# Measured durations in a list scheduler, one softplus table, and an addition by rows: the last two layers of a four-layer network

## The chip, the cores and the metric

The program runs on one core of a Trainium2 chip. A core has five engines that each take their instructions strictly in order: PE (TensorE, matrix products, which write to PSUM), DVE (VectorE), ACT (ScalarE, which evaluates functions from a loaded table), POOL (GpSimd) and SP (SyncE, which here issues the transfers). They wait for each other through semaphores. The metric is the device time of one execution in microseconds (us); lower is better.

## The reference, cut to what matters

Four layers work on four images of 192 channels and 56x56 pixels, all in float32. The first two are done in one stage of the kernel and are not touched. The third is a windowed attention with a gated feed-forward part, the fourth a selective scan over each image in four directions.

```python
# third layer: what follows the attention
def _hft(x, w, b):                       # depthwise 3x3 convolution as a gate
    ...
    return jax.nn.sigmoid(_dwconv3(a, w, b)) * x
z1, z2 = jnp.split(z, 2, axis=1)
z = z1 * _dwconv3(_ln_c(z2, sgn_g, sgn_b), sg_w, sg_b)
return x1 + _conv1x1(z, fc2_w, fc2_b)

# fourth layer
xs = jnp.stack([x_hw, x_wh, x_hw[..., ::-1], x_wh[..., ::-1]], axis=1)
x_dbl = jnp.einsum('kcd,bkdl->bkcl', x_proj_w, xs)
dts, Bv, Cv = jnp.split(x_dbl, [R, R + N], axis=2)
dt = jax.nn.softplus(jnp.einsum('kdr,bkrl->bkdl', dt_proj_w, dts) + dt_proj_b[None, :, :, None])
def step(h, inp):                        # N = 4 states a channel
    dt_t, u_t, B_t, C_t = inp
    h = jnp.exp(dt_t[..., None] * A) * h + dt_t[..., None] * B_t[:, :, None, :] * u_t[..., None]
    return h, jnp.einsum('bkdn,bkn->bkd', h, C_t)
y = ys[:, 0] + ys[:, 2, :, ::-1] + transposed(ys[:, 1]) + transposed(ys[:, 3, :, ::-1])
```

So every image is scanned along its rows forward and backward and along its columns forward and backward, and the four results are added up in `y`.

## The kernel before, in words

**The scheduler.** Both layers are written as many small generators (one for a chunk of rows, a window, a scan). Each yields, before a piece of work, the engine, an assumed duration, the tiles it takes and perhaps a table of ACT; then it issues the instructions. `Order.run` (from line 296) is a list scheduler that runs while the program is built: among all generators it takes the one whose next piece can start first by the assumed durations, plus 0.05 us times the generator's place in line, and advances that engine's assumed clock. The order of the instructions on each engine is thus fixed in the program, and the assumed durations do nothing but decide it. `on_dve(*n, ...)` assumes 0.08 + 0.00105 us times the elements, `on_pe(n)` 0.0019 us times the columns, `on_pool(n, each=...)` 0.2 + `each` times the elements.

**Layer 2** (the third layer; `layer2`). Bands of rows go through `front`, `quad` (attention of four windows) and `back`; chunks of eight rows go through `head` (the gate, with a depthwise convolution), `grow` (layer norms, L1195 and L1215, and the expansion, L1432) and `tail` (the second convolution, then the product L1497, PE's L1506 and the addition L1514). `dwconv` issues nine taps for each of two or three channel groups on DVE (L1341, L1343), one piece of work a tap.

**Layer 3** (the fourth layer; `layer3`). `begin(b, c)` takes a chunk of eight rows of image b: layer norm, projection (PE, L1821), the depthwise convolution as 18 matmuls with diagonal matrices (PE, L1851), SiLU, and `product` (PE, L1893), which makes dt, B and C for the two row directions and stores them. Once all chunks of an image are through, `begin_columns` calls `product` for the two column directions; its operand is a view of `u` that steps by 56 elements. `load` fetches these rows again (SP), `sizes` makes dt for two chunks at a time (PE L1985, ACT softplus L1997), `decay` spreads dt over four states by transfers (SP, L2023) and takes the exponential (ACT, L2031). `scan(t, h)` does one chunk for one half of the channels: du = dt u (DVE, L2046 by rows, L2049 by columns), three matmuls that spread it over the states (PE, L2056), three products with B (DVE, L2062), three scans (DVE, L2078), three products with C (POOL, L2085), the sum over the states (PE, L2101) and the addition to y (DVE, L2106, L2111 by rows and L2114 by columns). I call one such `scan` a half-step: an image has 56 (14 rows forward, 14 columns forward, 14 columns backward, 14 rows backward), the layer 224, counted from 0. `final(b, c)` is the last layer norm and output projection (L1770, L1789, L1929, L1940).

**The table of ACT.** A piece of work may name a table; the scheduler then issues a load of that table (L315) when it differs from the last. For softplus it names `softplus_and_others`. The built program of before holds, ahead of the softplus of L1997, 71 further loads at L1997's own line, which the compilation put there.

Of the kernel before, what the change touches and what calls it, by code (L numbers as in the profile page):

```python
# [19 lines left out]
B, C, H, W = 4, 192, 56, 56  # L20
HW = H * W
HALF = 96
CH = 448
# [302 lines left out]
    return "PE", 0.0019 * n, takes, None, ready  # L326


def on_dve(*n, takes=(), ready=None):
    return "DVE", sum(0.08 + 0.00105 * i for i in n), takes, None, ready  # L330


def on_scan(n, ready):
# [13 lines left out]


EXP_LN, GELU = "natural_log_exp_and_others", "gelu_and_others"
SILU, SOFTPLUS = "silu_and_others", "softplus_and_others"  # L350


def layers01(tc, x_in, packs, aps, dst):
# [723 lines left out]
def layer2(tc, src, packs, aps, dst):  # L1077
# [12 lines left out]
    with ExitStack() as ctx:  # L1090
# [242 lines left out]
        def dwconv(parts):  # L1333


            for t in range(9):
                yield on_dve(*(n * W for _, _, _, n, _, _ in parts))
                for dst, pad, i, n, wt, bias in parts:
                    x = pad[:, i + t // 3 : i + t // 3 + n, t % 3 : t % 3 + W]
                    if t == 0:  # L1340
                        nc.vector.tensor_scalar(dst, x, wt[:, 0:1], bias, ALU.mult, ALU.add)  # L1341
                    else:
                        nc.vector.scalar_tensor_tensor(dst, x, wt[:, t : t + 1], dst, ALU.mult, ALU.add)  # L1343
# [332 lines left out]
def layer3(tc, src, packs, aps, dst):  # L1676
# [8 lines left out]
    with ExitStack() as ctx:  # L1685
# [106 lines left out]
        def begin(b, c):  # L1792


            u = us[b % 2]

            yield lambda: (b, c) == (0, 0) or (gone("begun", b, c - 1) if c else gone("begun", b - 1, NCHUNK - 1))
            yield lambda: b < 2 or gone("scanned", b - 2)

            yield lambda: b == 0 or gone("multiplied", 8 * NSC * (b - 1) + 6 * c)  # L1800
            yield on_sp("row", "row")
            xl, xn = take("row"), take("row")
            nc.sync.dma_start(xl[:HALF], pixels(src[b])[:, :, c * CH : (c + 1) * CH])

            i = NCHUNK * b + c
            pad, above = pads[i % 2], pads[(i - 1) % 2]
            yield lambda: i < 2 or gone("convolved", i - 2)
            yield on_pool(200, 200)
            nc.gpsimd.memset(pad[:HALF, :, :, 0 : W + 2 : W + 1], 0.0)
            if c == 0:  # L1810
                nc.gpsimd.memset(pad[:HALF, :, 1], 0.0)
            else:
                nc.gpsimd.tensor_copy(pad[:HALF, :, 0:2, 1 : 1 + W], above[:HALF, :, 8:10, 1 : 1 + W])
            if c == NCHUNK - 1:
                nc.gpsimd.memset(pad[:HALF, :, 10], 0.0)
            yield from layer_norm(xl, xn, over=(xl,))

            def project(m):
                px = take()
                for k in range(2):  # L1820
                    nc.tensor.matmul(  # L1821
                        px[:HALF, :CH], inT[:, k, HALF * m : HALF * m + HALF], xn[:, k], start=(k == 0), stop=(k == 1)
                    )
                return px

            tiles = []
            for m in range(2):
                yield on_pe(2 * CH, "bank")
                tiles.append(project(m))
            for m in range(2):  # L1830
                yield on_act(CH)
                nc.scalar.activation(  # L1832
                    pad[:HALF, m, 2:10, 1 : 1 + W],
                    rows2(tiles[m][:HALF, :CH]),
                    AF.Identity,
                    bias=in_b[:, m : m + 1],
                )
                done(tiles[m])
            passed.add(("begun", b, c))
            y0, y1 = max(8 * c - 1, 0), 8 * c + (8 if c == NCHUNK - 1 else 7)  # L1840
            n = y1 - y0
            at = y0 - (8 * c - 1)
            px = slice(y0 * W, y1 * W)
            zt = None
            for h in range(2):
                pz = pc = None
                for t in range(9):
                    yield on_pe(n * W, *(("bank",) if t == 0 else ()), ready=order.end - 0.5 if t else None)
                    if t == 0:
                        pc = take()  # L1850
                    nc.tensor.matmul(  # L1851
                        rows2(pc[:HALF, : n * W]),
                        diag[:, h, t],
                        pad[:, h, at + t // 3 : at + t // 3 + n, t % 3 : t % 3 + W],
                        start=(t == 0),
                        stop=(t == 8),
                    )
                yield on_act(n * W)
                nc.scalar.activation(
                    u[:HALF, h, px], pc[:HALF, : n * W], AF.Identity, bias=w["c96.conv_b"][:, h : h + 1]  # L1860
                )
                done(pc)
                yield on_pe(2 * CH, "bank")
                pz = project(2 + h)
                yield on_act(CH, takes=() if h else ("gate",))
                if h == 0:
                    zt = take("gate")
                nc.scalar.activation(zt[:, h], pz[:HALF, :CH], AF.Identity, bias=in_b[:, 2 + h : 3 + h])
                done(pz)
            done(xn)  # L1870
            passed.add(("convolved", i))
            yield on_act(2 * n * W, 2 * CH, table=SILU)
            nc.scalar.activation(u[:HALF, :, px], u[:HALF, :, px], AF.Silu)
            nc.scalar.activation(zt, zt, AF.Silu)
            yield on_sp()
            nc.sync.dma_start(pixels(zmem[b])[:, :, c * CH : (c + 1) * CH], zt)
            done(zt)
            yield from product(b, 0, px, u[:, :, px])
            passed.add(("rows", b, c))

        def begin_columns(b, c):
            yield lambda: all(gone("rows", b, i) for i in range(NCHUNK))
            uv = us[b % 2].rearrange("p h (y x) -> p h x y", x=W)[:, :, 8 * c : 8 * c + 8]
            yield from product(b, 1, slice(c * CH, (c + 1) * CH), uv)
            passed.add(("columns", b, c))

        def product(b, o, px, u):

            n = px.stop - px.start
            yield on_pe(2 * n, "bank")  # L1890
            pp = take()
            for k in range(2):
                nc.tensor.matmul(pp[:40, :n], w["c128.xpT"][:, k, o], u[:, k], start=(k == 0), stop=(k == 1))  # L1893
            yield on_act(n, takes=("prod",))
            t = take("prod")
            nc.scalar.copy(t[:, :n], pp[:40, :n])
            done(pp)
            yield on_sp()
            nc.sync.dma_start(prods[b][o][:, px], t[:, :n])
            done(t)  # L1900
# [133 lines left out]
        def scan(t, h):  # L2034
# [5 lines left out]
            px = slice(c * SCH, (c + 1) * SCH)  # L2040
            yield lambda: t in sized and (2 * t + h == 0 or gone("multiplied", 2 * t + h - 1))
            dts, b_, c_ = sized[t]
            yield on_dve(SCH, takes=("du",))
            du = take("du")
            if o == 0:
                nc.vector.tensor_mul(du, dts[h], u[:HALF, h, px])  # L2046
# [20 lines left out]
            for j in range(3):  # L2067
                g = 3 * h + j
                yield lambda: (t, h, j) in decays and (head or (t - 1, g) in states)
                da, at = decays.pop((t, h, j))  # L2070
                yield on_scan(SCH, ready=max(at, ends[j]))
                sts.append(take("st"))
                r = slice(None, None, -1 if s else 1)
                first = 0.0
                if not head:
                    before = states.pop((t - 1, g))
                    first = before[:, 0:1] if s else before[:, SCH - 1 : SCH]
                nc.vector.tensor_tensor_scan(  # L2078
                    sts[j][:, r], da[:, r], tiles[j][:, :SCH][:, r], first, ALU.mult, ALU.add
                )  # L2080
                done(tiles[j])
                if not head:
                    done(before)
                yield on_pool(SCH, each=0.0021)
                nc.gpsimd.tensor_mul(da, sts[j], c_)  # L2085
                das.append(da)
                if last:
                    done(sts[j])
                else:
                    states[t, g] = sts[j]  # L2090
# [14 lines left out]
            if (o, s) == (0, 0):  # L2105
                nc.vector.scalar_tensor_tensor(  # L2106
                    y[:HALF, h, px], u[:HALF, h, px], d_sum[:, h : h + 1], sums, ALU.mult, ALU.add
                )
                started.add((t, h))
            elif o == 0:  # L2110
                nc.vector.tensor_add(y[:HALF, h, px], y[:HALF, h, px], sums)  # L2111
            else:
                yv = y[:HALF, h].rearrange("p (y x) -> p x y", x=W)[:, 8 * c : 8 * c + 8]
                nc.vector.tensor_add(yv, yv, rows2(sums, H))  # L2114
            done(py)
            added[b] += 1
            if o == 0 and s == 1 and h == 1:
# [54 lines left out]
```

## Time and profile before

| | us |
|---|---|
| median of three runs | 7017.2 |
| lowest and highest | 7013.4, 7018.1 |
| the profiled execution's own time | 7014.4 |
| its span | 7012.6 |
| layers 0 and 1: 0 to 2969 | 2969 |
| layer 2: 2969 to 4908 | 1939 |
| layer 3: 4908 to 7012.6 | 2105 |
| busy: PE, DVE, ACT, POOL | 5931.5, 5950.0, 2699.1, 1408.0 |
| table loads of ACT at L315 and at L1997 | 358 and 71 |

The boundaries of the layers are the times at which their weights are fetched. A group of instructions is shown with its line, engine, operation, tiles and shapes, its count, the busy time in us and the mean duration of one in ns; behind the last bar stands the idle time of its engine just before it and what ended it. Busy time counts overlap once, so it can be less than count times mean. A float32 matmul shows as two records of PE.

### The profile page before, as it was taken

To read this page: it belongs to the slowest core of one execution; us is meant where nothing else is said; L and a number is where in the kernel's file an instruction comes from. 1 tells how busy PE (TensorE), PEld (TensorE's weight loads), DVE (VectorE), ACT (ScalarE), POOL (GpSimd) and SP (SyncE) were. 2 spreads that over 40 slices of the span, in tenths; PEclk is the share of its full clock that TensorE was granted. 3 is DMA by queue.
4 is the path that set the end of the run, shared out by engine and by line. 5 is a ranking of instruction groups with operands and counts; after the bars stand their busy time and mean duration, and the time that the engine had idled before them with its cause. 6 is when DMAs were issued, how large, how long until landed. Compare 5 with 4: busy or idle time off the path is not lost.

```text
span 7012.6 us, 107574 instructions
## 1 busy us (share of the span) xinstructions
PE 5931.5 (85%) x43810; PEld 2703.5 (39%) x43810; DVE 5950.0 (85%) x7379; ACT 2699.1 (38%) x4134; POOL 1408.0 (20%) x1409
## 2 busy tenths in 40 slices
PE   4999989999999994877888888875888999888856
PEld 2444444444544441344444454442322322222212
DVE  2799999999999999548999989997269779698697
ACT  1111111222212221144455555553356666566544
POOL 0000000000000000032222122210235445355354
PEclk9999989999999997989999999997999999999977
DMA  3222112221222112210000000000246555465454
GB/s 93 56 52 68 31 32 60 52 68 29 63 51 66 35 43 70 64 32 16 17 20 15 19 16 19 18 13 7 60 116 152 135 130 147 115 151 147 118 131 112
DMA packets 252043, 462.68 MB, mean 66 GB/s; under 512 B 30388, under 2 KB 237964, under 8 KB 240412
## 3 DMA queue, kind: packets, MB, share of 16 engines
q1 hardware_dynamic: 251548, 455.80, 25.6%
q8 instruction: 345, 5.65, 0.3%
q14 instruction: 150, 1.23, 0.1%
HBM read 238.58 MB, written 62.96 MB: 43 GB/s over the span
## 4 chain that ended last, share of the span: by engine, by line
DVE 47%; PE 36%; issue 7%; ACT 5%; POOL 2%; DMA 2%; SPq 0%; DVEq 0%; POOLq 0%; ACTq 0%
DVE pr L789 9%; DVE oa L794 6%; PE a_bank L634 5%; DVE bg L1343 5%; PE c_bank L1851 4%; DVE ob L794 4%; DVE st L2078 3%; DVE bxn L1343 3%; PE c_bank L2056 2%; PE a_bank L884 2%; PE a_bank L869 2%; PE c_bank L1893 2%; PE c_bank L2101 2%; DVE c_bank L2062 2%; PE c_bank L1929 2%
## 5 line engine op out<-in xcount | busy, mean ns | idle before, releaser
L789 DVE TENSOR_TENSOR pr<-vdx,attn 112x1792 f32<-112x1792 f32 (+4 forms) x720 | 1185.9, 1649 | 19.0
L634 PE MATMUL a_bank<-qk_in,w_a 64*49 64x392 f32 x9408 | 1158.6, 496 | 0.0
L2085 POOL TENSOR_TENSOR da<-st,bc 128x448 f32<-128x448 f32 x672 | 845.4, 1267 | 884.9 <-DVE st L2078 793.7
L794 DVE TENSOR_TENSOR oa<-oa,pr 112x1792 f32<-112x1792 f32 (+1 forms) x423 | 765.1, 1809 | 0.0
L634 PE MATMUL a_bank<-qk_in,wd 64*49 64x392 f32 x4032 | 694.6, 496 | 0.0
L2078 DVE TENSOR_TENSOR_SCAN st<-da,st,c_bank 128x448 f32<-128x448 f32 x576 | 644.7, 1133 | 20.9 <-issue 12.7
L634 PEld LDWEIGHTS a_bank<-qk_in,w_a 64*49 64x49 f32 x9408 | 431.7, 120 | 395.9 <-issue 391.2
masks.py:197 POOL MEMSET b_ident<- 128x128 f32 x1 | 0.2, 206 | 2861.2 <-DVE sc L1042 2861.2
L2031 ACT ACTIVATE da<-da,a_neg 128x448 f32<-128x448 f32 x672 | 407.4, 658 | 155.8 <-DMA da<-dt 144.6
L315 ACT ACT_TABLE_LOAD x358 | 459.3, 1283 | 6.2
L2062 DVE TENSOR_TENSOR c_bank<-c_bank,bc 128x448 f32<-128x448 f32 x672 | 385.3, 619 | 75.3 <-PE c_bank L2056 74.5
L2056 PE MATMUL c_bank<-du,w_c 32*128 32x448 f32 x1344 | 291.3, 663 | 173.9 <-DVE du L2049 96.4
L1343 DVE SCALAR_TENSOR_TENSOR bg<-bzpad,w_b,bg 128x448 f32<-128x448 f32 (+2 forms) x672 | 421.8, 682 | 0.0
L1851 PE MATMUL c_bank<-pad,diag 128*96 128x448 f32 (+2 forms) x1008 | 413.0, 549 | 2.4 <-ACT pad L1832 2.4
L2101 PE MATMUL c_bank<-da,w_c 128*32 128x448 f32 x1344 | 343.8, 612 | 73.9 <-POOL da L2085 60.3
L794 DVE TENSOR_TENSOR ob<-ob,pr 112x1792 f32<-112x1792 f32 (+3 forms) x282 | 393.3, 1395 | 0.0
L869 PE MATMUL a_bank<-xc,w_a 128*128 128x448 f32 x672 | 300.8, 577 | 70.2 <-DVE xc L854 70.2
L878 ACT ACTIVATE hm<-a_bank,w_a 128x448 f32<-128x448 f32 x168 | 106.4, 634 | 644.9 <-PE a_bank L869 619.1
L634 PEld LDWEIGHTS a_bank<-qk_in,wd 64*49 64x49 f32 x4032 | 249.1, 120 | 256.4 <-issue 254.5
L1432 PE MATMUL bank<-bxn,w_b 128*128 128x448 f32 (+2 forms) x672 | 295.0, 567 | 16.7 <-DVE bxn L1215 16.3
L884 PE MATMUL a_bank<-hm,w_a 128*96 128x448 f32 x672 | 289.3, 562 | 21.1 <-ACT hm L878 21.1
L586 ACT ACTIVATE qk_in<-a_bank,qk_bias,qk_scale 64x224 f32<-64x224 f32 (+5 forms) x288 | 146.3, 526 | 412.2 <-PE a_bank L571 409.9
(306 smaller groups left out, 10091.6 us busy)
## 6 DMA issues: line engine op xcount, KB each, us to landing
da<-dt SPq DMA_DIRECT2D x672, 224.0 KB
vdx<-vmem SPq DMA_DIRECT2D x168, 476.0 KB
bc<-prod SPq DMA_DIRECT2D x224, 224.0 KB
row<-x SPq DMA_DIRECT2D x56, 336.0 KB
x<-x SPq DMA_DIRECT2D x4, 2352.0 KB
vmem<-vt SPq DMA_DIRECT2D x56, 168.0 KB
xc<-x SPq DMA_DIRECT2D x56, 168.0 KB
mid<-xc SPq DMA_DIRECT2D x56, 168.0 KB
```

What stands on the lines that cost most here:

```text
L315: self.nc.scalar.preload_act_table_set(table)
L634: nc.tensor.matmul(py[a][outs[g], : 7 * W].rearrange("p (y x) -> p y x", x=W), wt[halves[a], dx], q[halves[a], r, i0 + m : i0 + m + 7, dx ...
L789: nc.vector.tensor_mul(pr, vv, wt)
L794: nc.vector.tensor_add(og, og, before)
L869: nc.tensor.matmul(ph[:, :CH], w["a128.c1T"][:, k, 128 * m : 128 * m + 128], xt[:, k], start=(k == 0), stop=(k == 1),)
L1343: nc.vector.scalar_tensor_tensor(dst, x, wt[:, t : t + 1], dst, ALU.mult, ALU.add)
L1851: nc.tensor.matmul(rows2(pc[:HALF, : n * W]), diag[:, h, t], pad[:, h, at + t // 3 : at + t // 3 + n, t % 3 : t % 3 + W], start=(t == 0), ...
L2056: nc.tensor.matmul(tiles[j][:, :SCH], w["c96.rep"][r], du[r], start=True, stop=True)
L2062: nc.vector.tensor_mul(tiles[j][:, :SCH], tiles[j][:, :SCH], b_)
L2078: nc.vector.tensor_tensor_scan(sts[j][:, r], da[:, r], tiles[j][:, :SCH][:, r], first, ALU.mult, ALU.add)
L2085: nc.gpsimd.tensor_mul(da, sts[j], c_)
L2101: nc.tensor.matmul(py[32 * j : 32 * j + 32, :SCH], w["c128.sum"], das[j], start=True, stop=True)
```

## The change

Five durations that the scheduler assumes are altered; for 448 elements, a tap of a depthwise convolution goes from 0.550 to 0.618 us, du from 0.550 to 0.752 (rows) and 0.886 (columns), the product with C from 1.141 to 1.275, a column product on PE from 1.70 to 3.40. The table named for softplus is `softplus`, so that the load at L315 is the one that the activation needs. And the addition of the column results to y walks along the rows of y: y is read and written in runs of eight neighbouring elements, while the sums in PSUM are read with a step of 56 elements; before, y stepped by 56 and the sums were read straight.

```diff
-def on_dve(*n, takes=(), ready=None):
-    return "DVE", sum(0.08 + 0.00105 * i for i in n), takes, None, ready
+def on_dve(*n, takes=(), ready=None, each=0.00105):
+    return "DVE", sum(0.08 + each * i for i in n), takes, None, ready
...
-SILU, SOFTPLUS = "silu_and_others", "softplus_and_others"
+SILU, SOFTPLUS = "silu_and_others", "softplus"
...
             for t in range(9):
-                yield on_dve(*(n * W for _, _, _, n, _, _ in parts))
+                yield on_dve(*(n * W for _, _, _, n, _, _ in parts), each=0.0012)
...
-            yield from product(b, 0, px, u[:, :, px])
+            yield from product(b, 0, px, u[:, :, px], 2)
...
-            yield from product(b, 1, slice(c * CH, (c + 1) * CH), uv)
+            yield from product(b, 1, slice(c * CH, (c + 1) * CH), uv, 4)
...
-        def product(b, o, px, u):
+        def product(b, o, px, u, passes):
...
-            yield on_pe(2 * n, "bank")
+            yield on_pe(passes * n, "bank")
...
-            yield on_dve(SCH, takes=("du",))
+            yield on_dve(SCH, takes=("du",), each=0.0018 if o else 0.0015)
...
-                yield on_pool(SCH, each=0.0021)
+                yield on_pool(SCH, each=0.0024)
...
-                yv = y[:HALF, h].rearrange("p (y x) -> p x y", x=W)[:, 8 * c : 8 * c + 8]
-                nc.vector.tensor_add(yv, yv, rows2(sums, H))
+
+                yv = y[:HALF, h].rearrange("p (y x) -> p y x", x=W)[:, :, 8 * c : 8 * c + 8]
+                nc.vector.tensor_add(yv, yv, sums.rearrange("p (x y) -> p y x", y=H))
```

Since one line is added, the lines of the new kernel from 2113 on stand one lower.

## The prediction

> **What bounds the kernel now.** I first split the span by layer, in the view of busy time per stretch (columns: length; then busy us and instructions of PE, PE weight loads, DVE, ACT, POOL; granted PE clock; DMA share; GB/s). The first three lines are the layers; the other three are one image of the last layer: rows backward, rows forward of the next image, and its two column passes.
>
> ```profile
> 0.00:2969.00 2969.00, 2642.63 (x23294) 1285.26 (x23294) 2690.30 (x2135) 573.96 (x1061) 13.23 (x13) 0.95 0.22 54
> 2969.00:4908.00 1939.00, 1516.69 (x15012) 868.31 (x15012) 1663.13 (x3258) 942.13 (x1414) 453.28 (x619) 0.89 0.07 19
> 4908.00:7012.60 2104.60, 1772.17 (x5504) 549.94 (x5504) 1596.57 (x1987) 1183.00 (x1659) 941.47 (x777) 0.91 0.49 126
> ...
> 5409.00:5555.00 146.00, 133.13 (x421) 45.55 (x418) 107.84 (x139) 100.50 (x142) 62.30 (x50) 0.96 0.54 141
> 5555.00:5694.00 139.00, 126.43 (x366) 37.83 (x368) 94.77 (x123) 73.65 (x101) 54.30 (x52) 0.95 0.47 119
> 5694.00:5890.00 196.00, 169.83 (x590) 49.99 (x588) 189.66 (x231) 121.36 (x174) 110.31 (x90) 0.94 0.58 147
> ```
>
> The first layer is untouched. Layer 2 is DVE's (1663 of 1939 us). Layer 3 changes its bound twice an image: in the column passes DVE is busy 97% (189.7 of 196), in the row passes PE is (133 of 146, 126 of 139) while DVE idles about 80 of 285 us. Next, who DVE waits for, first in layer 2, then in layer 3 (total us, times, longest):
>
> ```profile
> DVE bxn L1215 <- ACT bank L1213: 40.3, 15, 5.5
> DVE bp L1514 <- PE bank L1506: 40.1, 26, 4.5
> DVE bacc L1655 <- PE bank L1639: 40.0, 18, 4.8
> DVE bzpad L1215 <- ACT bank L1213: 23.8, 11, 4.9
> ...
> DVE y L2106 <- PE c_bank L2101: 134.0, 25, 24.1
> DVE c_bank L2062 <- PE c_bank L2056: 74.5, 76, 8.0
> DVE row L1789 <- ACT c_bank L1787: 71.1, 22, 8.4
> ```
>
> All are waits for a chain through PE and ACT that the list scheduler thought covered. Then the groups of instructions that the diff names, and two pieces of the chain that ended last:
>
> ```profile
> L1343 DVE SCALAR_TENSOR_TENSOR bg<-bzpad,w_b,bg 128x448 f32<-128x448 f32 x480 | 299.7, 679 | 0.0
> ...
> L1997 ACT ACT_TABLE_LOAD x71 | 91.1, 1283 | 4.0 <-DVE st L2078 3.6
> ...
> L2049 DVE TENSOR_TENSOR du<-dt,u 96x448 f32<-96x448 f32 x112 | 113.6, 1014 | 0.0
> L2114 DVE TENSOR_TENSOR y<-y,c_bank 96x448 f32<-96x448 f32 x112 | 109.9, 982 | 12.9 <-PE c_bank L2101 12.6
> L2111 DVE TENSOR_TENSOR y<-y,c_bank 96x448 f32<-96x448 f32 x56 | 34.0, 607 | 30.6 <-PE c_bank L2101 30.6
> ...
> 5624.88 24.91 PE c_bank L1893 x32
> ...
> 5650.40 1.28 ACT L315
> ...
> 5651.69 1.28 ACT L1997
> ...
> 5652.98 0.64 ACT dt L1997
> ```
>
> A tap counts 299.7/480 = 0.624 us of DVE though one lasts 679 ns: neighbours overlap. The column products stand in one block of 24.91 us on PE (32 records: 14 column matmuls and 2 row matmuls, two records each), in which DVE waits 22.9 us. Behind it two table loads stand in a row before softplus.
>
> [...] The trace has the 1283, but the activation starts 0.01 us after the load, so I count 1.283. [...] du by columns, one hopping source, takes at best 947 ns, (947-140)/448 = 1.80; y by columns, source and destination hopping, 982 ns is 1.88 (140 ns is what L2111's 607 leaves over 448 x 1.042). Those streams are in SBUF. [...] No DVE instruction of the trace hops through PSUM.
>
> **The change, part by part.**
>
> *Taps in layer 2.* No instruction changes; the planner's 448-element tap goes from 0.08+0.00105x448 = 0.550 to 0.618 us, against 0.624 measured. The built order shows DVE's sequence with other interleaving. I summed the DVE work that stands in the order between a layer norm's subtraction and its multiplication, between the last product and L1514, and between the softmax's subtraction and L1655, by the durations above. In each class I took the length of chain at which the shortfalls of the old order add up to the waits measured between 3140 and 4650 us (23.9, 18.4, 19.1, 31.9 us; chains of 4.6 to 7.7 us), and applied it to the new order: layer norms lose about 10 us of shortfall, L1514 3.5, L1655 3; the reload after L1416 gains 3. With 6 us at the layer's two ends that is -20 us. Bounds: -40 (the shortfalls don't see that a wait removed also brings the next chain forward) and +10 (PE's own order is shuffled too).
>
> *Softplus table.* 71 loads of 1.283 = 91 us leave ACT, and the built order has 6 fewer switches besides. ACT is busy 1183 of 2105 us in layer 3, so only loads on the chain count: ten whole ones stand on it and three tails of 0.15, 13.3 us. What lies beside them takes over in part (DVE's scans, PE's convolution): -10, between 0 and -13.3.
>
> *y by rows.* 112 additions now hop in PSUM only; y is read and written in runs of 8. [...] They all stand in the column passes, which DVE bounds, but where the order has an addition as the last thing between du and L2062, PE's broadcast (du to L2062 took 1.4 to 2.3 us) swallows the saving; 70% gives -5. Ends: a free hop, 0.607 us, 112 x 0.375 = -42[...]. [...]
>
> *du, C products and column products in the planner.* du goes from 0.550 to 0.752 and 0.886 (0.856 and 1.014 measured), the C product on POOL from 1.141 to 1.275 (1.258), a column product from 1.70 to 3.40 us ((24.91-4x0.43)/7 = 3.31 measured). Durations change order, not work. In the built order the seven column products stand in one block at the same half-step (each image has 56: 14 rows forward, 28 columns, 14 rows backward), so the 22.9 us wait stays. What moves is the next image's convolution. Counting matmuls of one image (half-steps 70 to 126 of the layer's 224), the column passes hold 57 of L1851 before and 50 after; the rows backward 36 and 45. At 0.864 us each (18 records of the chain in 7.78 us; so for the other projections too, with 0.96 us for three broadcasts, 0.88 for three sums, 0.75 for a dt matmul and 3.31 for a column product) PE's work goes from 158 to 150 us in the column passes, where it was hidden by DVE, and from 128 to 138 us in the rows backward, where PE is the bound. It also stands in longer blocks: half-steps 97 and 98 hold 26.8 us of PE against 14.7 of DVE (before: 12.9 and 12.6), half-step 117 has 18 convolution matmuls in it. Taking the larger of PE's and DVE's work half-step by half-step, the sum grows by 9 us an image, 27 us over three. For the row passes of before this sum gives 286 us against 285 measured; for the columns it is too strict (209 against 196). So +16, between 0 and +27. No wait is added; the DMA issues of SP (L2023, L1970) keep their number; ACT waits 144.6 us for them in the layer, beside DVE's work.
>
> Sum: -20-10-5+16 = -19. The profiled execution took 7014.4 us around its span of 7012.6; the median of the runs is 7017.2, 2.8 higher. 7017.2-19 = 6998.
>
> **The rivals.** *The PSUM hop is free* (chance 0.26): y takes 0.61 us, -42 x 0.7 = -29 instead of -5, 6974. For it: the additions of L1655 read and write runs of 8 at 409 ns, no dearer than L1594's long ones at 410, so y itself is free of penalty. [...] *The blocks on PE decide* (0.25), the slower end: in half-steps 97-98 and 116-117 the excess of PE over DVE grows by 11.8 and 8.5 us, thrice each, 61 us if nothing is caught up later; against the 35 us of gains, +26, 7043. It decides from 5.8 us a block on. For it: DVE can't run ahead of PE by more than the next scans, and y L2106 waits behind just such a block today. Against it: the half-steps after are lighter. *Nothing that can be told* (0.07): the waits of layer 2 move rather than shrink and the rest cancels, 7015.
>
> **How the numbers follow.** My case has 0.42, with a range of its own from 6980 to 7013 us. A measurement of this kernel can tell about 0.2%, 14 us, from no change: faster ends at 7003, slower begins at 7031. My case is faster by 0.62 of its chance, the free hop by 0.95, together 0.51; slower is 0.85 of the blocks' case and a little of mine, 0.22; the rest, 0.27, is the same. Range: from 6955 (free hop, and layer 2 at its -40) to 7045 (blocks not caught up).
>
> **What would show it.** ACT with 71 loads fewer at L1997's line and none in a pair; y by columns at 0.9 us (0.6 if the hop is free, over 1 if the forecast fails there); DVE's waits in layer 2 for L1213, L1506 and L1639 20 us smaller; the column passes shorter by 2 to 3 us an image and the rows backward longer by 5 or so; L2106's wait behind the block still 23 us. It is wrong if layer 2 is not shorter than 1939 us, or if the row passes grow by more than 10 us an image.

## The result and the profile after

The changed kernel took 6990.8 us in the median (6988.4 to 6993.5, five runs) against 7017.2 us for the kernel before (7013.4 to 7022.3): 0.9963 of its time, 95% interval 0.9948 to 0.9978. That is 26 us less, 7 us below the 6998 forecast and inside its range. The forecast's sum was 19 us; the terms that make it up were not all right.

The profiled execution took 6988.4 us around a span of 6986.6. First the changed kernel's busy time per stretch, by layer, with the columns of the prediction (length; busy us and instructions of PE, weight loads, DVE, ACT, POOL; granted PE clock; DMA share; GB/s):

```profile
0.00:2969.50 2969.50, 2649.49 (x23294) 1283.69 (x23294) 2689.76 (x2135) 573.24 (x1061) 13.22 (x13) 0.95 0.22 54
2969.50:4909.10 1939.60, 1503.62 (x15012) 864.54 (x15012) 1671.73 (x3258) 940.57 (x1412) 443.96 (x619) 0.89 0.07 19
4909.10:6986.60 2077.50, 1763.92 (x5504) 540.16 (x5504) 1538.24 (x1987) 1091.34 (x1584) 947.80 (x777) 0.92 0.50 128
```

Layer 2 gained nothing (1939.0 to 1939.6). All of the gain is in layer 3, 2104.6 to 2077.5: DVE has 58 us less there, ACT 92 us less. To see which phase gained I cut layer 3 at du: a column pass runs from the first du by columns of an image to its first du of the backward rows (half-steps 14 to 41 of an image), a row pass from there to the next image's first du by columns. One image of the kernel before, columns and then rows:

```profile
5212.90:5409.30 196.40, 170.22 (x592) 50.32 (x592) 190.48 (x233) 121.84 (x175) 110.69 (x91) 0.95 0.59 148
5409.30:5693.60 284.30, 258.86 (x782) 82.92 (x780) 201.91 (x260) 173.86 (x241) 116.20 (x100) 0.96 0.50 130
```

and of the changed kernel:

```profile
5215.10:5404.30 189.20, 159.34 (x563) 46.21 (x563) 179.82 (x232) 114.54 (x169) 111.88 (x88) 0.92 0.61 152
5404.30:5696.40 292.10, 266.58 (x815) 85.41 (x812) 196.96 (x261) 156.29 (x227) 118.31 (x102) 0.95 0.49 127
```

The columns became 7.2 us shorter: DVE has 10.7 us less to do. The rows became 7.8 us longer: PE has 7.7 us more to do, the convolution that the columns no longer hold. Over the first three images the columns give 22 us and the rows take back 18 (the means stand in the table below). Most of the profit comes from the last image: its column pass and what follows went from 203.0 + 150.3 to 185.6 + 144.1 us.

The groups of the changed kernel that answer to those of before (count, then busy us, mean ns):

```profile
L315 ACT ACT_TABLE_LOAD x352 | 451.6, 1283 | 6.0
L1343 DVE SCALAR_TENSOR_TENSOR bg<-bzpad,w_b,bg 128x448 f32<-128x448 f32 x480 | 301.3, 682 | 0.0
...
L2049 DVE TENSOR_TENSOR du<-dt,u 96x448 f32<-96x448 f32 x112 | 113.1, 1010 | 0.0
...
L2115 DVE TENSOR_TENSOR y<-y,c_bank 96x448 f32<-96x448 f32 x112 | 67.7, 604 | 21.3 <-PE c_bank L2101 21.1
...
L2111 DVE TENSOR_TENSOR y<-y,c_bank 96x448 f32<-96x448 f32 x56 | 33.9, 606 | 45.7 <-PE c_bank L2101 45.7
```

The addition by columns, which reads PSUM with a step of 56 elements, takes 604 ns, as long as the one by rows that reads it straight (606); it was 982. The 71 table loads at the softplus's own line are gone, and L315 has the 6 fewer that the built order showed.

DVE's waits in layer 3 of the changed kernel (total us, times, longest):

```profile
DVE y L2106 <- PE c_bank L2101: 121.9, 22, 23.8
DVE c_bank L2062 <- PE c_bank L2056: 115.6, 89, 8.1
```

The wait behind the block of seven column products is still there, 23.8 us. The wait for the broadcast of du grew from 74.5 to 115.6 us. And DVE's waits in layer 2 of the changed kernel:

```profile
DVE bxn L1195 <- PE bank L1193: 62.1, 15, 28.0
DVE bp L1514 <- PE bank L1506: 37.8, 22, 4.8
DVE bxn L1215 <- ACT bank L1213: 34.1, 19, 4.8
DVE bzpad L1215 <- ACT bank L1213: 28.8, 13, 7.9
DVE bzpad L1195 <- PE bank L1193: 21.7, 7, 6.5
DVE bacc L1655 <- PE bank L1639: 20.5, 13, 3.6
...
DVE bacc L1308 <- ACT bacc L1306: 12.0, 10, 4.2
DVE bg L1341 <- ACT bzpad L1467: 11.2, 16, 1.7
```

beside the lines of before that the prediction did not show:

```profile
DVE bxn L1195 <- PE bank L1193: 56.1, 15, 27.8
...
DVE bzpad L1195 <- PE bank L1193: 12.6, 8, 2.5
...
DVE bacc L1308 <- ACT bacc L1306: 5.2, 8, 1.3
...
DVE bg L1341 <- ACT bzpad L1467: 2.6, 3, 0.9
```

The wait for L1639 is halved and those for L1213 and L1506 fall by 1.2 and 2.3 us, but those for L1193, L1306 and L1467 rise by 31 us together and take it over.

### The profile page after: what moved, and what is told of

Its sections match the earlier page's. It is cut to its first block, busy times and chain, and to the rows that moved or that the text cites. A ratio compares the mean times of both kernels' runs of the same rounds, so it can differ in the third digit from the quotient of the medians.

```text
span 6986.6 us, 107490 instructions
## 1 busy us (share of the span) xinstructions
PE 5917.0 (85%) x43810; PEld 2688.4 (38%) x43810; DVE 5899.7 (84%) x7379; ACT 2605.1 (37%) x4057; POOL 1405.0 (20%) x1409
## 5 line engine op out<-in xcount | busy, mean ns | idle before, releaser
L794 DVE TENSOR_TENSOR oa<-oa,pr 112x1792 f32<-112x1792 f32 (+1 forms) x423 | 764.8, 1808 | 0.0
L2062 DVE TENSOR_TENSOR c_bank<-c_bank,bc 128x448 f32<-128x448 f32 x672 | 382.7, 618 | 116.3 <-PE c_bank L2056 115.6
L2101 PE MATMUL c_bank<-da,w_c 128*32 128x448 f32 x1344 | 360.5, 601 | 93.1 <-POOL da L2085 82.5
L1343 DVE SCALAR_TENSOR_TENSOR bg<-bzpad,w_b,bg 128x448 f32<-128x448 f32 (+2 forms) x672 | 423.9, 686 | 0.0
L1851 PE MATMUL c_bank<-pad,diag 128*96 128x448 f32 (+2 forms) x1008 | 406.5, 545 | 0.2 <-ACT pad L1832 0.2
L794 DVE TENSOR_TENSOR ob<-ob,pr 112x1792 f32<-112x1792 f32 (+3 forms) x282 | 393.1, 1394 | 0.0
L2056 PE MATMUL c_bank<-du,w_c 32*128 32x448 f32 x1344 | 261.2, 642 | 124.2 <-DVE du L2049 68.8
```

What stands on the lines that cost most here:

```text
L794: nc.vector.tensor_add(og, og, before)
L1851: nc.tensor.matmul(rows2(pc[:HALF, : n * W]), diag[:, h, t], pad[:, h, at + t // 3 : at + t // 3 + n, t % 3 : t % 3 + W], start=(t == 0), ...
L2062: nc.vector.tensor_mul(tiles[j][:, :SCH], tiles[j][:, :SCH], b_)
L2101: nc.tensor.matmul(py[32 * j : 32 * j + 32, :SCH], w["c128.sum"], das[j], start=True, stop=True)
```

## The experiments

Each kernel is timed against the kernel before on the same chip. The table has the phases of layer 3 from one profile each: the mean of the first three column passes and of the three row passes, the last column pass together with what follows it, and PE's granted clock in the last column pass. Conv is the count of convolution matmuls (L1851) in half-steps 70 to 97 (columns), 98 to 111 (rows backward) and 112 to 125 (rows forward) of the built order.

| | us | ratio, 95% | columns | rows | last columns + rest | clock there | conv |
|---|---|---|---|---|---|---|---|
| before | 7017.2 | 1 | 196.6 | 285.5 | 353.3 | 0.74 | 57, 36, 33 |
| the change | 6990.8 | 0.9963 (0.9948-0.9978) | 189.2 | 291.5 | 329.7 | 0.86 | 50, 45, 31 |
| y alone | 6989.4 | 0.9952 (0.9939-0.9964) | 191.0 | 285.9 | 343.0 | 0.86 | 57, 36, 33 |
| table alone | 7016.4 | 0.9995 (0.9987-1.0003) | 197.0 | 285.8 | 355.7 | 0.72 | 57, 36, 33 |
| y, table | 6976.0 | 0.9937 (0.9924-0.9949) | 189.7 | 281.6 | 355.6 | 0.62 | 57, 36, 33 |
| du, C, column durations | 7039.5 | 1.0024 (1.0014-1.0033) | 197.4 | 296.3 | 342.4 | 0.87 | 50, 45, 31 |
| taps alone | 7021.2 | 1.0003 (0.9994-1.0011) | 196.7 | 288.0 | 353.8 | 0.73 | 57, 36, 33 |
| eight taps | 6973.4 | 0.9938 (0.9923-0.9953) | 196.7 | 288.0 | 354.3 | 0.73 | 57, 36, 33 |
| y, table, du, columns | 6929.0 | 0.9870 (0.9857-0.9884) | 182.6 | 279.6 | 331.8 | 0.84 | 60, 36, 30 |
| y, table, du | 6947.3 | 0.9895 (0.9881-0.9908) | 189.7 | 281.3 | 323.1 | 0.89 | 39, 54, 33 |
| y, table, spread | 6945.1 | 0.9892 (0.9878-0.9905) | 194.6 | 270.0 | 356.9 | 0.67 | 54, 45, 27 |
| the change, C 0.0023 | 6950.6 | 0.9906 (0.9891-0.9921) | 181.7 | 282.3 | 344.9 | 0.81 | 60, 36, 30 |
| the change, C 0.0025 | 6918.7 | 0.9862 (0.9845-0.9878) | 183.6 | 272.9 | 332.2 | 0.82 | 63, 36, 31 |
| spread, du, columns, C 0.0025 | 6832.1 | 0.9740 (0.9726-0.9755) | 183.5 | 255.6 | 327.0 | 0.92 | 56, 36, 24 |

Three kernels of the table leave layer 3 as it was (before, taps alone, eight taps), and their rows took 285.5, 288.0 and 288.0 us: a difference of 2 or 3 us between two profiles says nothing.

**The parts apart.** Four kernels with one part or two, the rest as before. Their edits are hunks of the change: the last one (y), the one of SOFTPLUS (table), both, and those of du, the C product and the column products (the three durations).

> The kernel before with the addition of the columns by rows alone; the order of the instructions is that of before. Theory A (the addition gives the gain and the new order takes part of it back): the addition takes 0.604 us as in the changed kernel, 112 x 0.378 = 42 us of DVE, of which 70 to 90% reach the end: 29 to 38 us faster, about 6983, the column passes 189 us or less instead of 196.5, the row passes unchanged at 284. Theory B (the new durations give the gain, the addition's saving is swallowed by the wait for PE's broadcast): at most 10 us faster.

> The kernel before with the softplus table alone; order as before, 71 table loads fewer. Both theories: 10 us faster (0 to 13), in the row passes and at the start of layer 3; ACT's busy time falls by 91 us. Rival: all of it is covered, no difference.

> The addition by rows and the softplus table, with all durations of the scheduler as before. Theory A: the sum of the two single runs, 39 to 48 us faster than before and thus 10 to 20 us faster than the changed kernel, 6970 to 6980, since the row passes keep their 284 us or less where the changed kernel has 292. Theory B: slower than the changed kernel, 6998 or more.

> Only the scheduler's durations of du, C product and column product, with the old addition, the old table and the old taps. Theory A: 9 convolution matmuls an image move from the column passes into the rows backward, three times, each half-step excess uncovered: 10 to 25 us slower, the row passes 292 us instead of 284, the column passes no longer than before. Theory B: 10 to 20 us faster.

Beside these four the kernel before took 7020.9 us. The addition by rows alone gives 31.5 us. Its group, in the profile of that kernel:

```profile
L2114 DVE TENSOR_TENSOR y<-y,c_bank 96x448 f32<-96x448 f32 x112 | 67.6, 604 | 18.9 <-PE c_bank L2101 18.9
```

112 x (0.982 - 0.604) = 42.3 us leave DVE, and three quarters of it (31.5/42.3 = 0.74) arrive in the time. They don't arrive evenly: DVE loses 10.6 us an image, and the first three column passes become 5.7 us shorter each, the last one 11.7, with PE's clock at 0.86 there instead of 0.74. The table alone can't be told from no change (4.4 us); on top of y it is worth 6989.4 - 6976.0 = 13.4 us. In the profiles this is a balance: 25 us are gained up to the last column pass, and 12.6 are lost in it and after it (343.0 to 355.6), where the clock falls from 0.86 to 0.62. The three durations cost 18.6 us. So y and table without any new duration are 15 us faster than the whole change, and the new order of layer 3 takes back part of what they give.

**Taps alone.** Is layer 2's part lost, or taken back elsewhere?

```diff
-                yield on_dve(*(n * W for _, _, _, n, _, _ in parts))
+                yield on_dve(*(n * W for _, _, _, n, _, _ in parts), each=0.0012)
```

> Only the planner's duration of a tap in layer 2 is changed; the order of layer 3 is as before, and so is every instruction. Theory 1 (formed after the result: the waits for L1639 and L1213 shrink, but the layer's end still comes after the same chain of head, projections and tail, so the time goes into other waits): layer 2 stays within 5 us of 1939 us, the kernel within 5 us of the one before, ratio 0.9993 to 1.0007. Theory 2 (the prediction's own step: 20 us less waiting of the vector engine is 20 us less time, and in the changed kernel something else took it back): layer 2 at 1919 us, ratio 0.9972.

No difference: 7021.2 us against 7020.2. Busy time in layer 2 of this kernel:

```profile
2970.30:4908.50 1938.20, 1510.48 (x15012) 868.69 (x15012) 1671.46 (x3259) 940.57 (x1412) 456.10 (x621) 0.89 0.07 19
```

DVE idles 1938.2 - 1671.5 = 266.7 us, 9 less than before (1939.0 - 1663.1 = 275.9), and is busy 8 us more with the same instructions. So the waits did shrink, by half of what I had worked out, and the instructions became longer by as much: hs<-hs at L1384 (224 of them) went from 28.5 to 31.8 us, the taps of L1343 together from 710.7 to 714.1.

**Eight taps.** How much of DVE's work in layer 2 reaches the time at all? The kernel before, without the ninth tap of both convolutions.

```diff
-            for t in range(9):
+            for t in range(8):
```

> The kernel before without the ninth tap of both depthwise convolutions of layer 2 (the output lacks it): 140 of the 1120 instructions of L1343 leave the vector engine, 140 x 0.635 us = 89 us of its 1663 us. Theory V (in layer 2 the vector engine's work sets the time, and its waits are leftovers that move): layer 2 shorter by 75 to 89 us, the kernel at 0.9875 to 0.989. Theory F (the chain of the last chunks of an image sets it, and takes up what the vector engine saves elsewhere): shorter by 20 to 60 us, ratio 0.9915 to 0.997.

6973.4 us, ratio 0.9938 (0.9923 to 0.9953). Layer 2 in this kernel's profile, and DVE's wait for the first product of the layer norm there:

```profile
2966.20:4859.10 1892.90, 1501.80 (x15012) 859.38 (x15012) 1591.12 (x3119) 936.32 (x1410) 477.68 (x621) 0.90 0.07 19
```

```profile
DVE bxn L1195 <- PE bank L1193: 72.4, 15, 27.8
DVE bxn L1215 <- ACT bank L1213: 46.2, 27, 5.6
```

Of 89 us of taps, DVE's busy time loses 72, its idle time gains 26 (275.9 to 301.8), and the layer loses 46: about half. Theory F's number holds. Half of the work taken from DVE in this layer comes back, as waits for other chains (26 us) and as busy time of what is left (89 - 72 = 17 us), and 20 us of waiting were too little to show. That it is the chain of the last chunks of an image that takes it up, as theory F had it, no run shows: the waits that grew are spread over the layer.

**Durations added one by one on y and table.** Only du and the column products, then only du.

```diff
-            yield on_dve(SCH, takes=("du",))
+            yield on_dve(SCH, takes=("du",), each=0.0018 if o else 0.0015)
...
-            yield on_pe(2 * n, "bank")
+            yield on_pe(passes * n, "bank")
```

> y by rows and the softplus table as in the changed kernel, and the planner's durations of du and of the column products, not that of the C product on POOL nor that of the taps. In the built order the column passes of an image then hold 60 convolution matmuls (57 with the old durations), the rows backward 36 (36) and the rows forward 30 (33). Theory A (what counts is how much convolution stands in the row passes, where PE is the bound): 3 matmuls of 0.864 us an image leave the row passes, 2.6 us, three times: 5 to 10 us faster than y and table alone, ratio 0.9925 to 0.993. Theory B (the longer durations of du as such put DVE's work too late, whatever the convolution does): the row passes grow by 10 us an image or so as in the run with the three durations, ratio 0.997.

> y by rows, the softplus table, and the planner's duration of du alone. In the built order the column passes hold 39 convolution matmuls (57), the rows backward 54 (36), the rows forward 33 (33). Theory A (convolution in the row passes counts): 18 matmuls more of 0.864 us, 15.6 us an image in the rows backward, and the column passes give little of it back because DVE bounds them: 30 to 50 us slower than y and table alone, ratio 0.998 to 1.001. Theory B (only blocks of twelve and more convolution matmuls in one half-step hurt; there are three here as with the old durations): as y and table alone, ratio 0.9937.

Both expectations fell, on the fast side: 6929.0 us with du and the column products, 6947.3 with du. With du alone, on y and table, 18 convolution matmuls an image move into the rows backward, and the time falls by 28 us instead of growing by 30 to 50. Busy time of that kernel in a column pass and the rows after it:

```profile
5207.50:5395.70 188.20, 157.86 (x553) 44.65 (x552) 179.22 (x232) 114.98 (x168) 112.36 (x88) 0.97 0.61 153
5395.70:5677.80 282.10, 265.04 (x822) 85.52 (x824) 200.32 (x262) 157.65 (x230) 117.28 (x102) 0.97 0.52 132
```

PE has 265.0 us of work in the rows, nearly as much as in the changed kernel (266.6), and they are 10 us shorter. PE idled 25 us in the rows with the old durations (281.1 - 256.0 in the kernel with y and table), and that idle time took up the 9 us. So the count of convolution matmuls in the row passes doesn't set the time.

Where du does gain is the last image's columns, where no convolution of a next image stands: in the profiles its 32 us lie there and in what follows (355.6 to 323.1). There the kernel with y and table, and the one with du besides:

```profile
6620.00:6822.50 202.50, 135.19 (x392) 30.81 (x392) 177.89 (x226) 82.88 (x126) 114.31 (x85) 0.62 0.53 130
```

```profile
6620.40:6800.40 180.00, 124.54 (x396) 25.73 (x392) 173.17 (x224) 85.88 (x128) 111.92 (x85) 0.89 0.57 146
```

The granted clock of PE is 0.62 and 0.89. The broadcasts of du in the same two stretches (min/median/max ns):

```profile
L2056 PE MATMUL c_bank<-du,w_c x168: 534/949/1112, 6621.3 to 6817.8; 32*128 32x448 f32 x168
```

```profile
L2056 PE MATMUL c_bank<-du,w_c x168: 534/638/1111, 6621.7 to 6796.9; 32*128 32x448 f32 x168
```

and DVE's wait for them goes from 18.5 to 4.9 us. With the old duration the order puts four dt matmuls (L1985) into one half-step and none into the next three; with the new one two and two. In these two passes the clock's records hold only 0.5 and 1.0, for 3.4 us at a time and multiples of it. PE stands still for longer than 3.4 us seven times in the first pass and twice in the second; its waits for du (L2049) add up to 43.3 and 20.9 us. Whether the stands bring the lower clock was not shown.

The order alone doesn't set the clock. The kernel with y alone has the same order on PE here, the four dt matmuls in one half-step and the seven long stands; it differs from the kernel with y and table only in the table loads on ACT. Its last column pass:

```profile
6645.10:6836.40 191.30, 109.83 (x394) 25.52 (x392) 176.60 (x226) 93.35 (x134) 114.42 (x85) 0.86 0.55 138
```

The clock is 0.86, the median of the broadcasts 638 ns, DVE's wait for them 9.3 us. So with PE's order held, the lower clock goes with 11 us (191.3 to 202.5), and the rest of the 22 us with the new order. All six kernels with the old order of layer 3 have between 0.62 and 0.86 there, and the kernel of the next experiment, with two and two dt matmuls and no stand over 3.7 us, has 0.67. What sets the clock between these is open.

**Spread.** The block of column products broken up.

```diff
         def begin_columns(b, c):
             yield lambda: all(gone("rows", b, i) for i in range(NCHUNK))
+            yield lambda: c == 0 or gone("multiplied", 8 * NSC * b + 6 + 2 * c)
```

> y by rows, the softplus table, all durations as before, and one added condition in begin_columns, so that the seven column products of an image follow one another over later half-steps instead of standing in one block of 25 us on PE. Four of the seven then stand in the column passes; the convolution moves too (54, 45 and 27 matmuls in columns, rows backward and rows forward, against 57, 36 and 33). Theory A (PE is the bound in the row passes): four products of 3.31 us leave the row passes and 3 matmuls of 0.864 us come in, 10.6 us an image, of which the columns, where DVE has 180 of 190 us, give back up to half: 15 to 30 us faster than y and table alone, ratio 0.9895 to 0.9915. Theory B (the 23 us wait of L2106 behind the block is lost time as a whole): 60 us faster or more, ratio 0.985. Theory C (the block only moves PE's work in time): no change, ratio 0.9937.

6945.1 us, 31 below y and table: theory A, by its number and its phases (rows 11.6 us shorter, columns 4.9 longer; 15 of the 31 us lie in the first image's rows, ahead of the table's phases). DVE's wait behind the block, in layer 3 of the kernel with y and table and of this one (where the lines are one higher):

```profile
DVE y L2106 <- PE c_bank L2101: 131.5, 25, 24.1
```

```profile
DVE y L2107 <- PE c_bank L2102: 59.5, 31, 4.2
```

The waits of over 20 us are gone and 72 us of waiting with them, of which 31, less than half, came out as time.

**The C product.** The run with y, table, du and columns differs from the change only in the taps, which are worth nothing, and in the C product; it is 62 us faster. Is a long C product bad, or the order that 0.0024 happens to give?

```diff
-                yield on_pool(SCH, each=0.0024)
+                yield on_pool(SCH, each=0.0023)
```

> The changed kernel, with the planner's C product on POOL at 0.0023 us an element instead of 0.0024. In the built order the column passes of an image then hold 60 convolution matmuls, the rows backward 36 and the rows forward 30, as in the run with y, table, du and columns (the changed kernel: 50, 45, 31), but 18 of them still stand in one half-step at the 12th and 6th half-step before the rows' end, the latter just ahead of the seven column products, as in the changed kernel. Theory D (that block just ahead of the column products costs 10 us an image, the count costs the column passes 6 us an image): row passes 290 us, column passes 183 us, 20 us faster than the changed kernel, ratio 0.993. Theory A (the count alone): as the run with y, table, du and columns, ratio 0.987. Theory E (a long C product in the planner is bad in itself): between the two by its size, 0.99 or so.

> The changed kernel, with the planner's C product on POOL at 0.0025 us an element instead of 0.0024, further from the old 0.0021. In the built order the column passes hold 59 to 63 convolution matmuls, the rows backward 36, the rows forward 27 to 31, and no half-step of the rows holds 18: the two groups ahead of the column products stand in two half-steps. Theory D (the block decides): row passes 281 us, column passes 183 us, 6930 us, ratio 0.987. Theory E (a long C product in the planner is bad in itself): no faster than the changed kernel, ratio 0.996 or more.

With 0.0025 (the same line) the kernel is 72 us below the change, the fastest median of all durations that were tried, though its interval overlaps that of the run with the old C product: theory E falls. Theory D has its number there (0.987), but not its reason: half-step 60, and 172 likewise, holds 18 convolution matmuls all the same. The images differ in this kernel: the row passes take 268.3, 284.5 and 266.0 us, the column passes 181.7, 187.4 and 181.7, and the counts in the table are those of the slow image. With 0.0023 theory D falls by its phases, and A by its number (0.9906 for 0.987); theory E's number fits, which 0.0025 rules out. The columns and rows with 0.0023 in the profile:

```profile
5211.10:5392.80 181.70, 163.82 (x586) 50.24 (x585) 178.78 (x231) 116.80 (x171) 114.18 (x91) 0.99 0.64 160
5392.80:5675.60 282.80, 256.98 (x789) 81.11 (x788) 196.12 (x262) 156.59 (x227) 116.58 (x99) 0.96 0.49 130
```

The rows are 282.8 us and not 290, although 18 convolution matmuls stand in half-step 117 as in the changed kernel. From the start of half-step 100 to that of 126 the two take the same, 267.4 and 267.8 us. What differs is what stands before: half-steps 70 to 97 take 181.7 against 189.1 us, and 98 and 99 together 15.1 against 24.3. Of these 17 us, 5 have gathered by the start of half-step 97, spread over the columns, where the changed kernel's clock is lower (0.92 against 0.99 in the image shown); 12 fall between there and half-step 100. In the changed kernel 18 matmuls stand in half-steps 97 and 98, the last two convolution groups, put off to the end of the columns; here 8 stand in 97 and none in 98. The kernel with y and table says the same of the rows: its half-steps 98 and 99 take 13.5 us, and from 100 to 126 it takes 267.5. It isn't that place alone: with y, table and du 18 stand in half-steps 98 and 99, which take 18.2 us, and the image is 10 us shorter than in the changed kernel. What makes it cheap there is open. Of the remaining 21 us between this kernel and the one with the old C product, 13 lie after the third image's rows (344.9 against 331.8 us), where the clock is 0.81 against 0.84, and 8 in the three row passes.

**All together.** Spread with du, the column products and C at 0.0025, and the old duration of the taps.

> The changed kernel with the old duration of the taps, the C product at 0.0025 and the column products of an image spread over later half-steps by the added condition. If the two gains add (spread alone gave 31 us on y and table, the durations of du and columns 47): 6898 us, ratio 0.9826. If the spread no longer gains where no block stands ahead of the column products, or PE's work (423 us an image of 464) leaves no room: 6930 us, ratio 0.987.

6832.1 us, 0.9740 of the kernel before, more than the two gains added (6898). One image of it, columns and rows (the shortest of its row passes; the mean is 255.6), and the wait that stood at 121.9 us in the changed kernel (lines are one higher from L1883 on):

```profile
5625.50:5808.70 183.20, 167.19 (x589) 48.73 (x588) 180.68 (x233) 120.22 (x175) 113.22 (x90) 0.98 0.63 158
5808.70:6060.80 252.10, 234.32 (x758) 74.31 (x758) 201.99 (x262) 157.23 (x226) 115.13 (x100) 0.96 0.56 147
```

```profile
DVE y L2107 <- PE c_bank L2102: 47.7, 26, 5.5
```

In the rows PE needs 234.3 us instead of 266.6 and waits less besides (17.8 us instead of 25.5); the spread moves products into the columns, where DVE hides them. Part of the rest may be the clock: over the columns PE's work has 0.98, in the changed kernel 0.92. How much each gives isn't settled.

## Why the prediction was right, and where it wasn't

The time was right to 7 us by luck: two errors of over 20 us cancel. The parts as measured are 0 for the taps, -31.5 for y, -13.4 for the table on top of it and +14.8 for the order, together -30.1 (against 7020.9 us for the kernel before in those runs); the prediction had -20, -5, -10 and +16.

*Taps in layer 2, -20: wrong, 0.* The step that failed takes the shortfalls of the chains for time. In the stretch from 3140 to 4650 us the wait for L1213 fell by 10.6 us, as worked out; that for L1639 fell by 19.9 instead of 3, that for L1506 by 0.3 instead of 3.5. But over the whole layer those for L1193, L1306 and L1467 rose by 31 together (56.1 + 12.6 + 5.2 + 2.6 = 76.5 to 107.0), DVE's idle time fell by 8 (275.9 to 267.9), and its busy time grew by as much. Even saved work, with eight taps, passes only to one half. The prediction named "layer 2 not shorter than 1939" as what would make it wrong; it was not shorter (1939.6). Why the other chains take the waits over is open.

*y by rows, -5: mis-sized, 31.5 us.* That work leaves DVE in the column passes and reaches the time in part was right; the price of the hop was not. The -5 supposes 0.9 us for an addition, which no run of this case shows. It takes 604 ns with the hop in PSUM, against 606 for the straight read, so the hop costs nothing here. A hop in SBUF does cost: du takes 947 ns at best by columns, with u hopping, and 591 by rows (L2049 and L2046), and the addition took 982 with y hopping. (The 1.042 ns an element behind the prediction's 140 ns is near what L794 shows, 1083 ns for 896 elements and 2016 for 1792: (2016-1083)/896 = 1.041.) The free end of the bound, -42 us, stood in the text, and so did the pass-through of 70%: 0.74 measured over all, but 5.7 of 10.6 us in an ordinary column pass, so that this too owes something to the last one. The rival "the PSUM hop is free" had the mechanism; its 6974 missed by 17 us because it carried the 20 us of layer 2 with it.

*Softplus table, -10: inside its bounds, not well tested.* 4 us alone, where the interval ends at 9, and 13 on top of y, as the balance of a gain of 25 and a loss of 12.6 that the sum of the loads on the chain doesn't hold. The 71 loads went as said.

*Order of layer 3, +16: total right, composition wrong.* Measured +18.6 alone, and 6990.8 - 6976.0 = +14.8 on y and table (the taps included; 18 by the two ratios, since the kernels were timed at different times). In the profiles of these last two kernels it is +30 in the three row passes (291.5 - 281.6 each) and -26 in the last column pass and after it, with the start of the layer and the other layers making the rest. I had 9 us an image in the rows and nothing at the end. The reason given for the rows, 0.864 us for each convolution matmul that comes in, gives the right size here and fails with du alone, where 18 come in at no cost. The gain at the end goes with the granted clock (0.62 to 0.86), which the sum left out. Of the 26 us, 17 lie in the last column pass (202.5 to 185.6), and y alone shows that 11 of these can come with the clock and no new order at all; the kernel that the order is measured against here is the one with the lowest clock. That the total came out is luck.

*The blocks on PE.* Of the two places that this rival named, half-steps 97 and 98 are where the changed kernel loses: 98 and 99 take 24.3 us instead of the 13.5 with y and table. Half-step 117 with its 18 convolution matmuls costs nothing: from 100 to 126 the two take 267.8 and 267.5 us. Gains elsewhere were larger than the rival allowed, so it did not end slower.

## What to carry to other kernels

A measured duration in a list scheduler is not always a better one: the duration of the C product at 0.0021, 0.0023, 0.0024 and 0.0025, with the other new durations of layer 3 in place, gave 6929, 6951, 6991 and 6919 us, because each shuffles the order anew; try the order, not the truth of its costs, and keep what a small sweep finds fastest. Take edits that remove work (the addition by rows, the loads) apart from those that only reorder, or the second hide the first. And where one engine stands in a long block of one kind of work, try a condition that spreads it: here it was worth 31 us with the old durations, and 87 us on top of the fastest new ones (6918.7 to 6832.1), where the durations gave 57 at best (6976.0 to 6918.7) and cost 15 as first chosen.

## What the runs showed of the hardware

DVE read PSUM with a step of 56 float32 at the rate of a straight read: 604 against 606 ns for 448 elements in the changed kernel. And the clock granted to PE differed under the same order: with the same matmuls in the same order and nearly the same DVE work (176.6 and 177.9 us), the last columns ran at 0.86 with y alone or 0.62 with y and table and took 191.3 or 202.5 us. A new order brought 0.89 and 180.0 us; the evenness of the order didn't foretell the clock (0.67 in the kernel with y, table and spread).
